# Two unread products at the start, a split gate pair, and a second set of rows turned earlier

## The chip, the cores and the metric

The kernel runs on one core of a Trainium2 chip. A core has a matrix engine (TensorE, PE), a vector engine (VectorE, DVE), a scalar engine (ScalarE, ACT), a general engine (GpSimd, POOL), and a queue engine (SyncE, SP) that mostly issues transfers. Products go to PSUM, a small accumulator memory, and are read from there by VectorE and ScalarE. The metric is the device time of one execution in microseconds (us).

## The reference

Two layers work on x, 8 sequences of 256 rows of 512 numbers, with a context of the same size.

```
x = x + long_convolution(ctx, ctx, layernorm(x))      # 32 heads of 8 x 2 halves, filter of 512
x = x + ternary_ffn(layernorm(x))                     # 512 -> 2048 -> 512, quantised rows and weights
x = x + cross_attention(layernorm(x), ctx)            # 16 heads of 32
x = x + experts(layernorm(x))                         # 2 shared experts, best 2 of 16 routed ones
```

An expert is `w2(gelu(g(x)) * w1(x))` with 256 hidden columns. The router takes the sigmoid of `x @ wa`, keeps the two best experts of each row and weighs their outputs by the two affinities divided by their sum. Everything is float32 apart from the quantised products.

## The kernel before

The program is one long stream for each engine. Inside each stage `in_order` fixes the order of TensorE, VectorE, ScalarE and GpSimd to that of the program text; transfers on SP may be placed by the scheduler. Engines meet through semaphores, and a tile is reused when its last reader is done. A pool's tag with `bufs=n` has n such slots.

**Start.** `first_norm` (L544) takes mean and variance of the first half of the rows, eight tiles of 128 x 512 as they land (`moment`, L149 and L150). Then ScalarE normalises tiles 0 to 3 and VectorE tiles 4 to 7, alternately. PE turns each normalised tile with four 128 x 128 transposes (`transposed`, L162) into a PSUM tile of the tag `tr`, which has two slots. The engine that normalised the tile copies it to `qT` (L537). Up to here PE has had nothing to do. The convolution follows: for each head PE forms `y` (L691) from the filter `tp` and products `kv` of context columns, which GpSimd prepares (L629), and VectorE multiplies and adds.

**Expert stage, shared part.** `gate(tb, e, f, w, k)` (L1468) is half a gate pair: four products of 128 x 512 into a PSUM tile of the tag `gh`, which has four slots. Half 0 is what goes through Gelu, half 1 is the factor. `gated` (L1480) takes the Gelu of half 0 on ScalarE (L1483) and multiplies on VectorE (L1484). tb counts blocks of 512 rows, e the shared experts, f the halves of the hidden columns. `down` (L1488) multiplies back and adds to the rows.

The routing runs in between, as a generator, `route` (L1512), advanced by `next(pieces)`. Its pieces are, in order: the affinities; the best expert; the second best; `both`, the sum of the two choices (L1540); the ranks, where PE counts for each row and expert how many rows came before (17 small products, L1544 to L1550) and VectorE turns counts into places; the slots; then one piece for each of the 16 row tiles. A row piece normalises the tile on VectorE (`dxs`, L1437) and has GpSimd scatter it twice to a table `xd` in HBM (L1600), and scales the rows (L1608). Four pieces have been taken when the loop of the remaining six pairs begins; it does a whole pair, then `gated`, then 2, 3, 3, 3, 3, 2 pieces:

```
    for (tb, e, f), n in zip(rest, (2, 3, 3, 3, 3, 2)):
        gated(tb, e, f, gate_up(tb, e, f, shw[e]), yTs[tb])
```

**Routed part.** A `Unit` (L1625) is one routed expert with up to 256 of its rows. Building it loads its weights and its rows `xr` from `xd` (L1635). The tag `xr` has two slots. `turn` transposes the rows, 8 transposes into two `gh` tiles, and ScalarE copies them to `xT` (L1643). `products` forms the hidden columns (L1656, Gelu L1662, factor L1663), `back` the output (L1672), which goes to a table `yd`. A `Double` (L1681) holds rows of two experts that overflowed; five of them are put among the units, the first at place 3. The loop builds unit i+1, runs the products of unit i, turns unit i+1, then does `back` of unit i-1. Only the first unit is turned ahead of the loop. Afterwards the shared experts of blocks 2 and 3 run while GpSimd gathers rows of `yd`.

Of the kernel before, what the change touches and what calls it, by code (L numbers as in the profile page):

```python
# [8 lines left out]
F32 = mybir.dt.float32  # L9
# [9 lines left out]
B, S, D = 8, 256, 512  # L19
# [59 lines left out]
def tile_kernel(ctx: ExitStack, tc: tile.TileContext, a: dict, out: bass.AP):  # L79
    nc = tc.nc  # L80
# [24 lines left out]
    xs = const.tile([P, 2, B, D], F32, name="xs")  # L105
# [17 lines left out]
    def rsqrt(v, eps, n, name):  # L123

        ve = stat.tile([P, n], F32, tag="rs_ve", name=f"{name}_ve")
        nc.scalar.activation(ve, v, AF.Identity, bias=eps)
        s = stat.tile([P, n], F32, tag="rs_s", name=f"{name}_s")
        nc.scalar.activation(s, v, AF.Sqrt, bias=eps)

        def rest():  # L130
            r0 = stat.tile([P, n], F32, tag="rs_r0", name=f"{name}_r0")
            nc.vector.reciprocal(r0, s)
            return newton(ve, r0, n, name)

        return rest

    def newton(ve, r0, n, name):
        t = stat.tile([P, n], F32, tag="rs_t", name=f"{name}_t")
        nc.vector.tensor_tensor(t, r0, r0, ALU.mult)
        nc.vector.tensor_tensor(t, t, ve, ALU.mult)  # L140
        nc.vector.scalar_tensor_tensor(t, t, -0.5, r0, ALU.mult, ALU.mult)
        r = stat.tile([P, n], F32, tag="rs_r", name=f"{name}_r")
        nc.vector.scalar_tensor_tensor(r, r0, 1.5, t, ALU.mult, ALU.add)
        return r

    def moment(dst, t, name):

        st = stat.tile([P, 6], F32, tag="bn", name=f"{name}_bn")
        nc.vector.bn_stats(st, t)  # L149
        nc.vector.bn_aggr(dst, st)  # L150
# [31 lines left out]
    pp = psA.__enter__()  # L182
# [351 lines left out]
    def turned(xn, nm, t0):  # L534

        ps = transposed(pp, xn, nm, "tr", PERM)
        return lambda copy: copy(qT[:, :, t0 : t0 + P], ps)  # L537

    def minus_mean(mv, r, n, name):
        nmr = stat.tile([P, n], F32, tag="nmr", bufs=2, name=name)  # L540
        nc.vector.scalar_tensor_tensor(nmr, mv[:, :, 0], -1.0, r, ALU.mult, ALU.mult)
        return nmr

    def first_norm():  # L544


        by_act, by_dve = (
            fp.tile([P, 4, D], F32, tag="big", bufs=4, name=f"xn0_{q}") for q in range(2)
        )
        mv = stat.tile([P, B, 2], F32, tag="mv0", bufs=1, name="ln0_mv")  # L550
        for b in range(B):
            moment(mv[:, b, :], xs[:, 0, b, :], f"ln0_{b}")
        r = rsqrt(mv[:, :, 1], ln_eps, B, "ln0")()
        nmr = minus_mean(mv, r, B, "ln0_nmr")
        copies = []
        for i in range(4):
            nc.scalar.activation(
                by_act[:, i, :], xs[:, 0, i, :], AF.Identity, bias=nmr[:, i : i + 1],
                scale=r[:, i : i + 1],
            )  # L560
            copies.append((turned(by_act[:, i, :], f"q0_{i}", i * S), nc.scalar.copy))
            j = 4 + i
            nc.vector.tensor_scalar(
                by_dve[:, i, :], xs[:, 0, j, :], mv[:, j, 0:1], r[:, j : j + 1],
                ALU.subtract, ALU.mult,
            )
            copies.append((turned(by_dve[:, i, :], f"q0_{j}", j * S), nc.vector.tensor_copy))
            if i:
                for _ in range(2):
                    to_place, copy = copies.pop(0)  # L570
                    to_place(copy)
        for to_place, copy in copies:
            to_place(copy)
# [167 lines left out]
    b1c = stat.tile([P, FC], F32, tag="b1c", bufs=1, name="b1c")  # L741
    nc.sync.dma_start(b1c, a["w1b"].rearrange("(p c) -> p c", p=P))
    first_norm()
    following = kv0, rows_of(0, nc.vector.tensor_copy)
    unfinished = None
# [414 lines left out]
    with tc.tile_pool(name="att", bufs=2) as ap_, tc.tile_pool(  # L1160
        name="psC", bufs=2, space=PSUM
# [217 lines left out]
    def weights(names, e, name, gu=None):  # L1379
        if gu is None:  # L1380
            gu = gate_weights(names, e, name)
        w2 = experts.tile([P, EC, D], F32, tag="w2", bufs=4, name=f"{name}_w2")
        nc.sync.dma_start(w2, of_expert(names[2], e).rearrange("(c p) f -> p c f", p=P))
        return gu, w2
# [3 lines left out]
    shw = [weights(shared_names, e, f"s{e}", None if e else gu0) for e in range(SH)]  # L1388
# [79 lines left out]
    def gate(tb, e, f, w, k):  # L1468
        ps = pd.tile([P, TB], F32, tag="gh", name=f"gu{k}{e}_{tb}{f}")
        for c in range(DC):  # L1470
            nc.tensor.matmul(  # L1471
                ps, lhsT=w[0][:, c, k, f * P : (f + 1) * P], rhs=xTs[tb][:, c, :],
                start=(c == 0), stop=(c == DC - 1),
            )
        return ps

    def gate_up(tb, e, f, w):
        return gate(tb, e, f, w, 0), gate(tb, e, f, w, 1)

    def gated(tb, e, f, gu, yT):  # L1480
        gp, up = gu
        ge = mo.tile([P, TB], F32, tag="ge", bufs=2, name=f"ge{e}_{tb}{f}")
        nc.scalar.activation(ge, gp, AF.Gelu, bias=gb[:, e, f : f + 1])  # L1483
        nc.vector.scalar_tensor_tensor(  # L1484
            yT[:, e, f, :], up, eb1[:, e, f : f + 1], ge, ALU.add, ALU.mult
        )
# [12 lines left out]
    def hidden_rows(tb):  # L1499
        return mo.tile([P, SH, EC, TB], F32, tag="yT", bufs=2, name=f"yT_{tb}")  # L1500
# [244 lines left out]
    pieces = route()  # L1745
    yTs = [hidden_rows(tb) for tb in range(2)]
# [5 lines left out]
    first_gate = gate(0, 0, 0, shw[0], 0)  # L1752
# [9 lines left out]
    first_gate = gate(0, 0, 1, shw[0], 0)  # L1762
# [6 lines left out]
    for _ in range(3):  # L1769
        next(pieces)  # L1770
    rest = [(tb, e, f) for tb in range(2) for e in range(SH) for f in range(EC)][2:]
    for (tb, e, f), n in zip(rest, (2, 3, 3, 3, 3, 2)):
        gated(tb, e, f, gate_up(tb, e, f, shw[e]), yTs[tb])
        for _ in range(n):
            next(pieces)

    for tb in range(2):
        for j in range(TB // P):
# [9 lines left out]
    order = [lambda e=e: Unit(f"r{e}", e, NS * P * e, NS * P) for e in range(E)]  # L1788
    for j in range(NO1 // 2):
        order.insert(4 * j + 3, lambda j=j: Double(j))  # L1790
    units = [order[0]()]
    units[0].turn()
    for i in range(len(order)):
        if i + 1 < len(order):
            units.append(order[i + 1]())
        units[i].products()
        if i:
            units[i - 1].turn_back()
        if i + 1 < len(order):
            units[i + 1].turn()  # L1800
        if i:
            units[i - 1].back()
        if i < NTT:
            nc.gpsimd.tensor_tensor(tile_of(i), tile_of(i), srow, ALU.add)
# [15 lines left out]
    shw = [weights(shared_names, e, f"t{e}") for e in range(SH)]  # L1820
# [105 lines left out]
```

## Time and profile before

| what | value |
|---|---|
| runs | 1160.84, 1160.36, 1160.26; median 1160.36 us |
| profiled execution | 1161.17 us, span 1159.4 us |
| mean granted TensorE clock | 0.995 |
| PE busy, 0 to 20.6 us (start) | 5.86 us |
| PE busy, 20.6 to 198 us (convolution) | 169.18 of 177.4 us |
| PE busy, 745 to 860 us (end of attention, shared experts, routing) | 110.44 of 115 us |
| PE busy, 860 to 1070 us (routed experts) | 208.81 of 210 us |

The profile is of one execution. The span runs from the first to the last instruction of the core; the execution's own time is 1.8 us longer. Times inside it count from the start of the span. PE's weight loads are listed apart (PEld) since they overlap products. An f32 product appears as two records, so the four products of half a pair are eight. "Idle before" an instruction is how long its engine had done nothing, and the name behind it is what that instruction waited for last. The chain that ended last is followed back from the end of the program.

### The profile page before, as it was taken

To read this page: it belongs to the slowest core of one execution; us is meant where nothing else is said; L and a number is where in the kernel's file an instruction comes from. 1 tells how busy PE (TensorE), PEld (TensorE's weight loads), DVE (VectorE), ACT (ScalarE), POOL (GpSimd) and SP (SyncE) were. 2 spreads that over 40 slices of the span, in tenths; PEclk is the share of its full clock that TensorE was granted. 3 is DMA by queue.
4 is the path that set the end of the run, shared out by engine and by line. 5 is a ranking of instruction groups with operands and counts; after the bars stand their busy time and mean duration, and the time that the engine had idled before them with its cause. 6 is when DMAs were issued, how large, how long until landed. Compare 5 with 4: busy or idle time off the path is not lost.

```text
span 1159.4 us, 16491 instructions
## 1 busy us (share of the span) xinstructions
PE 1099.6 (95%) x5866; PEld 661.3 (57%) x5885; DVE 679.2 (59%) x1499; ACT 525.3 (45%) x1181; POOL 440.8 (38%) x501
## 2 busy tenths in 40 slices
PE   4999998899988999999999999899999999999997
PEld 3777775454544565555555555554456766675443
DVE  5998999789874565755757656437612122222352
ACT  4437545888883466555556566631011221111000
POOL 5788887144321233333434335312770000000650
PEclk9999999999999999999999999899999999999999
DMA  7424420799400100000000010052667999997571
GB/s 270 153 74 155 145 83 13 255 302 291 116 1 1 55 1 1 20 19 1 20 8 12 2 37 1 1 193 83 238 207 251 312 340 326 294 320 245 153 251 39
DMA packets 122780, 153.25 MB, mean 132 GB/s; under 512 B 7482, under 2 KB 81274, under 8 KB 122179
## 3 DMA queue, kind: packets, MB, share of 16 engines
q1 hardware_dynamic: 108608, 116.49, 31.8%
q10 hardware_dynamic: 8962, 18.85, 4.5%
q0 software_dynamic: 5120, 16.78, 4.3%
q8 instruction: 49, 0.80, 0.3%
q14 instruction: 41, 0.33, 0.1%
HBM read 107.66 MB, written 44.43 MB: 131 GB/s over the span
## 4 chain that ended last, share of the span: by engine, by line
PE 74%; DVE 16%; POOL 4%; ACT 2%; issue 2%; DMA 0%; SPq 0%; POOLq 0%; DVEq 0%; ACTq 0%
PE r_h L1656 10%; PE gu L1471 9%; PE y L691 5%; PE pt L1222 5%; PE fo L1251 5%; PE v_mm L863 5%; PE r_po L1672 5%; PE q_mm L863 5%; PE po L1493 5%; PE k_mm L863 4%; PE sc L1186 2%; PE f_hp L399 2%; PE o L1241 2%; DVE f_hmax L433 2%; PE f_op L471 2%
## 5 line engine op out<-in xcount | busy, mean ns | idle before, releaser
L1211 POOL TENSOR_TENSOR pr<-pr,rden 128x1024 f32<-128x1024 f32 x64 | 121.3, 1895 | 155.2 <-DVE rden L1209 140.0
L691 PE MATMUL y<-kv,tp 128*128 128x288 f32 x640 | 161.7, 408 | 5.2 <-DVE wl L714 5.0
L691 PEld LDWEIGHTS y<-kv,tp 128*128 128x128 f32 x640 | 119.0, 190 | 42.5 <-PE y L691 10.0
L1202 ACT ACTIVATE pr<-sc,mx 128x256 f32<-128x256 f32 x256 | 118.6, 485 | 8.1 <-DVE mx L1194 7.0
L1809 POOL DMA_INDIRECT yg<-yd,slot x32 | 33.4, 1044 | 224.1 <-PE gu L1471 206.3
L1656 PE MATMUL r_h<-r_xT,r_gu 128*128 128x256 f32 x512 | 113.7, 380 | 1.4 <-ACT r_xT L1643 1.4
L1656 PEld LDWEIGHTS r_h<-r_xT,r_gu 128*128 128x128 f32 x512 | 96.8, 190 | 22.4 <-issue 8.0
L1194 DVE TENSOR_REDUCE mx<-sc 128x4 f32<-128x1024 f32 x64 | 77.5, 1213 | 4.8 <-PE sc L1186 4.8
L1222 PE MATMUL pt<-ident,pr 128*128 128x128 f32 x512 | 71.5, 282 | 6.6 <-ACT xT L1281 3.5
L1663 DVE SCALAR_TENSOR_TENSOR r_y<-r_h,eb,r_ge 128x256 f32<-128x256 f32 x32 | 15.5, 484 | 97.3 <-PE r_h L1656 97.3
L1222 PEld LDWEIGHTS pt<-ident,pr 128*128 128x128 f32 x512 | 55.6, 142 | 25.2 <-issue 15.4
L1227 ACT COPY pts<-pt 128x512 f32<-128x512 f32 x64 | 37.9, 592 | 70.1 <-PE pt L1222 70.1
L1662 ACT ACTIVATE r_ge<-r_h,gb 128x256 f32<-128x256 f32 x32 | 15.2, 474 | 108.9 <-PE r_h L1656 108.9
L399 PE MATMUL f_hp<-w1q,f_xq 128*128 128x512 bf16 x245 | 59.4, 379 | 5.3 <-ACT f_xq L376 4.5
L629 POOL TENSOR_TENSOR kv<-kx 128x2048 f32<-128x2048 f32 x16 | 57.6, 3602 | 12.8 <-ACT kx L615 12.8
L1251 PE MATMUL fo<-Wo_sb,oT 128*128 128x512 f32 x128 | 59.3, 607 | 0.0
L863 PE MATMUL k_mm<-Wk_sb,cx 128*128 128x512 f32 x128 | 58.2, 598 | 0.8 <-DVE xs L479 0.8
L471 PE MATMUL f_op<-w2q,f_hq 128*128 128x512 bf16 x249 | 57.7, 382 | 0.5 <-issue 0.2
L863 PE MATMUL v_mm<-Wv_sb,cx 128*128 128x512 f32 x128 | 57.7, 593 | 0.0
L1672 PE MATMUL r_po<-r_w,r_y 128*128 128x512 f32 x128 | 57.7, 593 | 0.0
L863 PE MATMUL q_mm<-Wq_sb,xT 128*128 128x512 f32 x128 | 57.6, 593 | 0.0
L1483 ACT ACTIVATE ge<-gu,gb 128x512 f32<-128x512 f32 x16 | 11.0, 688 | 102.4 <-PE gu L1471 100.0
(486 smaller groups left out, 2108.7 us busy)
## 6 DMA issues: line engine op xcount, KB each, us to landing
xd<-blank SPq DMA_DIRECT2D x1, 15360.0 KB, 59.4
tp<-kpd SPq DMA_DIRECT2D x32, 256.0 KB, 3.3
r_gu<-in_rg SPq DMA_DIRECT2D x16, 512.0 KB, 6.3
r_gu<-in_rw SPq DMA_DIRECT2D x16, 512.0 KB, 6.7
r_w<-in_rw SPq DMA_DIRECT2D x16, 512.0 KB, 6.8
r_xr<-xd SPq DMA_DIRECT2D x16, 512.0 KB, 6.9
yd<-r_yo ACTq DMA_DIRECT2D x32, 256.0 KB, 5.8
yd<-blank SPq DMA_DIRECT2D x1, 6144.0 KB, 78.1
```

Source lines behind the costliest of these rows:

```text
L399: nc.tensor.matmul(dst, lhsT=self.xq[:, i, c, :], rhs=w1q[:, c, cols], start=(c == 0), stop=False)
L471: nc.tensor.matmul(op, lhsT=self.hq[i][:, c, :], rhs=w2q[:, c, :], start=(c == 0), stop=(c == FC - 1))
L691: nc.tensor.matmul(y[:, ll, :, 0:PAIRS], lhsT=tp[:, dl : dl + P], rhs=view(kv, (m0 * G + hh) * PAIRS, [[G * PAIRS, B], [1, PAIRS]]), start ...
L863: nc.tensor.matmul(t, lhsT=lT[:, c, i * P : (i + 1) * P], rhs=w[:, c, :], start=(c == 0), stop=(c == DC - 1),)
L1194: nc.vector.tensor_reduce(self.mx, self.sc.rearrange("p r c k -> p (r c) k"), AX.X, ALU.max, negate=True)
L1202: nc.scalar.activation(self.pr[:, h // 2, h % 2, :], self.sc[:, h // 2, h % 2, :], AF.Exp, bias=self.mx[:, h : h + 1], accum_out=self.den[ ...
L1211: nc.gpsimd.tensor_tensor(flat, flat, rden.unsqueeze(2).to_broadcast([P, 4, S]), ALU.mult)
L1222: nc.tensor.transpose(pt[:, cc, k, :], self.pr[:, rr, cc, k * P : (k + 1) * P], ident)
L1251: nc.tensor.matmul(fo, lhsT=oT[:, c, :], rhs=wsb["Wo"][:, c, :], start=(c == 0), stop=(c == DC - 1))
L1471: nc.tensor.matmul(ps, lhsT=w[0][:, c, k, f * P : (f + 1) * P], rhs=xTs[tb][:, c, :], start=(c == 0), stop=(c == DC - 1),)
L1656: nc.tensor.matmul(ps, lhsT=self.w[0][:, c, k, f * P : (f + 1) * P], rhs=self.xT[:, c, 0:n], start=(c == 0), stop=(c == DC - 1),)
L1672: nc.tensor.matmul(po, lhsT=self.y[:, f, i * P : (i + 1) * P], rhs=self.w[1][:, f, :], start=(f == 0), stop=(f == EC - 1),)
```

## The change

The diff has three parts.

1. In `first_norm`, after the moments of tiles 5 and 6, PE multiplies the two moment columns with the tile of 512 columns, into a PSUM tile of the tag `tr`. Nobody reads the result.
2. In the loop of the remaining pairs the pieces stand between half 0 and half 1 of the pair instead of behind `gated`, and their numbers are 0, 2, 3, 3, 3, 3, and 2 behind the loop. As a result the same pieces come at the same place for VectorE, ScalarE and GpSimd. On PE the ranks now come after half 0 of the pair (0, 1, 1), where before they came ahead of it.
3. The second routed unit is built and turned ahead of the loop, behind the first. In the loop's first pass nothing is built or turned. On PE its transposes move ahead of the first unit's products, on ScalarE its two copies ahead of the first unit's two Gelus. On SP the first gate-weight load of the fourth routed expert comes behind the load of the first `Double`'s rows instead of ahead of it.

```diff
         for b in range(B):
             moment(mv[:, b, :], xs[:, 0, b, :], f"ln0_{b}")
+            if b in (5, 6):
+
+                nc.tensor.matmul(
+                    pp.tile([2, D], F32, tag="tr", name=f"idle{b}"), lhsT=mv[:, b, :],
+                    rhs=xs[:, 0, b, :], start=True, stop=True,
+                )
...
-    for (tb, e, f), n in zip(rest, (2, 3, 3, 3, 3, 2)):
-        gated(tb, e, f, gate_up(tb, e, f, shw[e]), yTs[tb])
+    for (tb, e, f), n in zip(rest, (0, 2, 3, 3, 3, 3)):
+        first_gate = gate(tb, e, f, shw[e], 0)
         for _ in range(n):
             next(pieces)
+        gated(tb, e, f, (first_gate, gate(tb, e, f, shw[e], 1)), yTs[tb])
+    for _ in range(2):
+        next(pieces)
...
-    units = [order[0]()]
-    units[0].turn()
+    units = []
+    for i in range(2):
+        units.append(order[i]())
+        units[i].turn()
     for i in range(len(order)):
-        if i + 1 < len(order):
+        if 0 < i < len(order) - 1:
             units.append(order[i + 1]())
         units[i].products()
         if i:
             units[i - 1].turn_back()
-        if i + 1 < len(order):
+        if 0 < i < len(order) - 1:
             units[i + 1].turn()
```

## The prediction

> **What bounds the kernel now.** I read the page's busy shares first, then the chain that ended last, then TensorE's timeline where the diff touches it, and last the other engines and the clock there.
>
> ```profile
> PE 1099.6 (95%) x5866; PEld 661.3 (57%) x5885; DVE 679.2 (59%) x1499; ACT 525.3 (45%) x1181; POOL 440.8 (38%) x501
> PE 74%; DVE 16%; POOL 4%; ACT 2%; issue 2%; DMA 0%; SPq 0%; POOLq 0%; DVEq 0%; ACTq 0%
> ```
>
> TensorE (PE) is busy for 95% of the span and is 74% of the chain; no DMA is on it. A microsecond taken off PE where the chain runs on PE should therefore come off the end. Rows of that chain in order of time (start, us, what):
>
> ```profile
> 14.36 3.58 PE q L162 x16
> ...
> 20.14 0.66 PE q L162 x4
> 20.80 7.29 PE y L691 x30
> ...
> 873.78 0.87 PE r_xTp L162 x8
> ```
>
> The first 16 transposes take 3.58/16 = 0.22 us each, late ones 0.87/8 = 0.11: PE starts at half speed. TensorE's timeline (start, duration, then idle before and its releaser):
>
> ```profile
> 784.22 7.11 PE L1471 MATMUL gu<-xT,s_gu 128*128 128x512 f32 x16
> 793.18 0.28 PE L1544 MATMUL rank<-both,ones 128*128 128x272 bf16 x1 [1.85 <-DVE both L1540]
> ...
> 794.27 34.50 PE L1471 MATMUL gu<-xT,s_gu 128*128 128x512 f32 x80
> ...
> 857.83 7.17 PE L1656 MATMUL r_h<-r_xT,r_gu 128*128 128x256 f32 x32 [0.72 <-ACT r_xT L1643]
> 864.84 1.04 PE L162 MATMUL r_xTp<-ident,r_xr 128*128 128x128 f32 x8
> 866.61 7.17 PE L1656 MATMUL r_h<-r_xT,r_gu 128*128 128x256 f32 x32 [0.72 <-ACT r_xT L1643]
> ```
>
> PE stands for `both` before the ranks, and twice for ScalarE's copies of turned rows. The granted clock, in windows cut on its own edges (window, length, PE busy, clock, DMA share, GB/s):
>
> ```profile
> 348.60:352.01 3.41, 0.67 (x5) 1.00 0.00 0
> 352.01:355.42 3.41, 3.19 (x15) 0.50 0.00 0
> 737.71:741.13 3.42, 1.67 (x13) 1.00 0.00 0
> 741.13:744.54 3.41, 3.41 (x5) 0.50 0.02 5
> ```
>
> After a thin window the clock is half for exactly one window of 3.413 us. The edges 352.01, 724.06 and 741.13 all lie on one grid; carried back it has edges at 10.68, 14.09 and 17.50. The start's weight loads fall from 0.23 to 0.14 us at about 17.4, so that is the same grid (the clock column reads 1.00 there: it shows no state before its first event).
>
> **Part 1, two products ahead of the first transposes.** They wait for the moments of rows 5 and 6, whose rows end at 9.96 and 10.75. A 128x512 f32 product is 0.86 us at full clock (an output projection's 4 products take 3.44), so 1.72 at half; with that price, of rows with 128 output columns, they run from 10.0 to 13.43. The first transpose at 14.36 is not held up. VectorE gets no wait from them, and their two PSUM slots come free on PE itself. A loss I exclude because of the 0.9 us in between.
>
> What a full clock from 14.36 is worth: VectorE's rows turn one behind the other, since two PSUM slots serve two engines. A warm round is PE 0.66 + copy 0.69 + handovers 0.07 = 1.42. The first of that lane issues at 14.36 + 0.44 = 14.80, the fourth at 14.80 + 3 x 1.42 = 19.06 instead of 20.14: 1.08 saved. A round at half is 1.11 + 0.69 + 0.07 = 1.87 with 0.43 more at either end: all-cold would be 2.2 behind warm. So the bounds are 0 (clock not lifted) and 2.2 (a run whose grid keeps all of this stage cold). With the edges of this run the products fill 2.75 of 3.41 us in the window 10.68 to 14.09. Rises that the trace shows come after 3.14 to 3.41; the clock is kept at 1.38 (222.3 to 225.7), dropped at 2.13 in small products. 2.75 lies nearest to the rises: I take 1.1.
>
> Behind it: the convolution `y` is PE's until 28 us and then alternates with VectorE. The second rows have landed by 21.5 (DMA share 0), are read at 31.0; `tp` and `kgs` are issued when PE or ScalarE frees a slot, so they move along. The third `kv` stands 3.5 us after its input. I let the 1.1 run through.
>
> [...]
>
> **Part 2, ranks between the halves of a pair.** Only four products move on PE: the first half of pair (0,1,1) goes ahead of the ranks. No other engine's order changes. Before: the 16 records of pair (0,1,0) issue until 784.22 + 16 x 0.43 = 791.09, ranks 793.18, next pair 794.27. After: first half 791.09 to 794.53; `both` ended at 793.03, so the ranks go at once, 794.53 to 795.62; second half at 795.62, where it was 794.27 + 3.44 = 797.71. Saved 2.09; the profile's idle of 1.85 (behind a modelled end) is the low bound; I take 2.0.
>
> The price: ranks reach VectorE 1.35 later. Its slots end at 799.81 + 1.35 = 801.16.
>
> ```profile
> 801.42 0.75 DVE L1484 SCALAR_TENSOR_TENSOR yT<-gu,eb,ge 128x512 f32<-128x512 f32 x1 [1.61 <-PE gu L1471]
> ```
>
> Here VectorE idled 1.61 for the second half, which now ends at 799.3, so this product starts at 801.16, 0.26 earlier. The scatters behind it are GpSimd's, 32 at 1.27 us, and keep their time less 0.26. Both PSUM slots the moved half needs were freed by 787.7.
>
> **Part 3, second expert's rows turned behind the first's.** Before: 8 transposes issue in 0.87 (856.07 to 856.94), products at 857.83; again 865.71 to 866.61. After: the second eight fill 856.94 to 857.81 while ScalarE copies the first pair (done 857.79), and the second unit's products follow the first's. Saved 0.89 + 0.90 = 1.79; the idle column gives 2 x 0.72 = 1.44 as the low bound; I take 1.8. ScalarE's two copies (1.07) move ahead of the first Gelu, which waits for PE until 859.87 anyway. The four `gh` slots suffice: the third is needed at 861.2, its copy ends at 858.4.
>
> What parts 2 and 3 need is that the rows are there. PE reaches them at 856.07 - 2.09 = 853.98, the second unit's at 854.85.
>
> ```profile
> 846.60 0.89 SPq L1635 DMA_DIRECT2D r_xr<-xd  x2
> ```
>
> and among the transfers of that stretch, with their median time to landing:
>
> ```profile
> r_xr<-xd SPq DMA_DIRECT2D x2, 512.0 KB, 4.1
> ```
>
> Issued 846.6 and 847.1; the first alone landed 3.6 after, so the second 4.6: 850.2 and 851.7, less 0.26. Some 3 us remain. On SP one load changes place: the fourth routed expert's gate weights go behind the overflow rows `o_xr`, which wait for the second rows' transposes, now at 857.8, still ahead of the end of the first unit's products (864.8) that those weights waited for. They are needed at 895. The units' other loads hang on PE and move with it; PE waits for no DMA from 860 to 1070.
>
> **Sum.** 1.1 + 2.0 + 1.8 = 4.9. The profiled execution took 1161.17 (span 1159.4 and 1.8 around it): it would be 1156.3. It stands 0.8 above the median of the runs, 1160.36, so I predict 1155.5. Low bounds 0 + 1.85 + 1.44 = 3.3 give 1157.1; high ones 2.2 + 2.09 + 1.79 = 6.1 give 1154.3.
>
> [...] A 4-product output projection at 741 took 5.13 on the chain against 3.44: a half-clock window on such work costs 1.7, and one may come or go when the stages shift by 1.1.
>
> **The rivals.**
> - *The clock is not lifted in time* (products of two columns count for little, or 80% of a window is too little): parts 2 and 3 alone, 1160.36 - 3.8 = 1156.6. For it: no rise in the trace after less than 3.14 us. Against: the clock was kept after windows with 1.38 and 1.51 us of busy PE, all of it wide products.
> - *The scatters become the bound*: PE comes earlier but the rows do not, and part 2 is given back: 1157.4. For it: GpSimd issues without a pause until 844.8. Against: 3 us of slack.
> - *Slower*: the second rows, now ahead of the first unit's products, land late and hold everything. PE loses the landing less 854.85; it is as slow as before at a landing of 859.8, and at 862.4 the time is 1163. That is 15 us after issue; the longest of all 16 row loads took 9.1, and 1157 would be the price of that.
> - *The stages take it back*: 28 to 357 us alternates between engines, and thin windows drop the clock. Two more half-clock windows on dense products take 3.4: 1158.9, no change within 0.2%.
>
> **How the numbers follow.** Forecast 0.62, clock not lifted 0.20, scatters 0.07, taken back 0.06, slower 0.05. The forecast's own range is 1154.0 to 1157.0. The first two hold 0.82; with bounds 1154.3 and 1157.1, and part of a half-clock window either way, the range is 1153.5 to 1157.8. A measurement of this kernel tells about 0.2% (2.3 us) from no change: faster is below 1158.0. The first three cases lie below that (0.89, of which 0.01 is left to the noise), the fourth within: faster 0.88, same 0.07, slower 0.05.
>
> **What would show it.** Part 1: weight loads of the first transposes at 0.14 us, q's fourth VectorE tile at 19.1, `y` 1.1 earlier. Part 2: no idle before the ranks, pair (0,1,1) split around them, VectorE's 1.61 gone. Part 3: 16 transposes in a row, no ScalarE wait before either unit's products. Wrong would be: loads still at 0.23 at 14.4; PE idle before `r_xTp` on a DMA; new windows at clock 0.50.

## The result and the profile after

The changed kernel took 1156.40 us (median of 6 runs, 1153.92 to 1157.90) against 1160.31 for the kernel before (6 runs), a ratio of 0.9963 with a 95% interval of 0.9953 to 0.9972: 3.9 us less by the medians, where 4.9 was forecast, and inside the range of 1153.5 to 1157.8. The interval stands for 3.2 to 5.5 us, so it holds the 4.9 too. The profiled execution, the slowest of the six, took 1157.9 (span 1156.1), 3.3 less than the profiled one of before, so it is read against that. The line numbers cited from here on are 6 higher than before behind L552, in every kernel that keeps the products of part 1.

The page of the changed kernel, busy time by engine and the chain by engine:

```profile
PE 1105.1 (96%) x5870; PEld 662.5 (57%) x5889; DVE 679.1 (59%) x1499; ACT 525.2 (45%) x1181; POOL 441.4 (38%) x501
PE 75%; DVE 16%; POOL 3%; ACT 2%; issue 2%; DMA 0%; SPq 0%; POOLq 0%; DVEq 0%; ACTq 0%
```

The bound has not changed: PE carries the chain. PE's timeline of the changed kernel (start, duration, idle before in brackets), at the start, around the ranks, and at the routed rows:

```profile
10.19 3.57 PE L555 MATMUL idle<-xs,ln_mv 128*2 128x512 f32 x4 [10.19 <-DVE ln_mv L150]
14.50 6.72 PE L162 MATMUL q<-ident,xn 128*128 128x128 f32 x32 [0.74 <-issue]
...
784.97 10.55 PE L1477 MATMUL gu<-xT,s_gu 128*128 128x512 f32 x24
795.35 0.28 PE L1550 MATMUL rank<-both,ones 128*128 128x272 bf16 x1
...
796.44 31.06 PE L1477 MATMUL gu<-xT,s_gu 128*128 128x512 f32 x72
827.34 27.63 PE L1499 MATMUL po<-s_w,yT 128*128 128x512 f32 x64
854.81 1.91 PE L162 MATMUL r_xTp<-ident,r_xr 128*128 128x128 f32 x16
856.57 14.08 PE L1662 MATMUL r_h<-r_xT,r_gu 128*128 128x256 f32 x64
```

The ranks stand between two blocks of products with no bracket: the wait of 1.85 for `both` is gone. Sixteen transposes run in a row, the products of both units follow, and the two waits of 0.72 for ScalarE are gone. Nothing waits for the rows.

Where the 3.3 us came from, by starts on PE (before, after): `lgT`, the first transposes for the router, 759.05 and 759.80, a loss of 0.75; the first `r_xTp` 856.07 and 854.81, so a gain of 2.01 between these two; the first `r_po` 874.49 and 871.36, a gain of 1.87 more. The rest of the program ends as much earlier, within 0.14. The start itself lost: `y` begins at 21.06, where it was 20.64. The granted clock of the changed kernel in windows cut on its edges (window, length, PE busy, weight loads, VectorE, ScalarE, GpSimd, clock, DMA share, GB/s):

```profile
8.73:12.14 3.41, 1.95 (x3) 0.34 (x4) 2.86 (x8) 0.32 (x2) 2.71 (x2) 1.00 0.45 160
12.14:15.55 3.41, 2.67 (x7) 1.08 (x6) 1.95 (x8) 1.70 (x3) 0.00 (x0) 1.00 0.98 237
15.55:18.97 3.42, 3.42 (x17) 2.66 (x15) 1.74 (x3) 2.60 (x4) 0.00 (x0) 1.00 0.99 378
...
193.05:196.46 3.41, 1.41 (x13) 0.81 (x11) 3.30 (x11) 1.48 (x3) 2.86 (x13) 1.00 0.01 2
196.46:199.87 3.41, 2.28 (x5) 0.89 (x7) 2.01 (x5) 1.12 (x2) 3.04 (x8) 0.50 0.00 0
199.87:203.29 3.42, 3.42 (x13) 2.33 (x12) 2.69 (x9) 1.43 (x3) 1.48 (x8) 0.50 0.19 23
```

The window of 3.413 us is the same, but its edges are elsewhere: in the profile of before they lie 0.44 after multiples of 3.413 us from the start of the span, here 1.90 after. The transposes' weight loads take 1.57 for eight up to 18.8 and 0.42 for four from 19.12: the clock rose at 18.97, where in before it was 17.50. And two half-clock windows stand behind a thin one at 196.46, where before had none. Between the start and the last microseconds, before has three half-clock windows (from 352.01, 724.06 and 741.13), the changed kernel five (two from 196.46, one from 227.18, two from 353.48).

### The profile page after: what moved, and what is told of

Read it like the earlier page. It is cut to its first block, busy times and chain, and to the rows that moved or that the text cites. A ratio compares the mean times of both kernels' runs of the same rounds, so it can differ in the third digit from the quotient of the medians.

```text
span 1156.1 us, 16504 instructions
## 1 busy us (share of the span) xinstructions
PE 1105.1 (96%) x5870; PEld 662.5 (57%) x5889; DVE 679.1 (59%) x1499; ACT 525.2 (45%) x1181; POOL 441.4 (38%) x501
## 4 chain that ended last, share of the span: by engine, by line
PE 75%; DVE 16%; POOL 3%; ACT 2%; issue 2%; DMA 0%; SPq 0%; POOLq 0%; DVEq 0%; ACTq 0%
PE r_h L1662 10%; PE gu L1477 10%; PE y L697 5%; PE pt L1228 5%; PE v_mm L869 5%; PE r_po L1678 5%; PE q_mm L869 5%; PE fo L1257 5%; PE po L1499 5%; PE k_mm L869 4%; PE sc L1192 2%; PE f_hp L399 2%; PE o L1247 2%; DVE f_hmax L433 2%; PE f_op L471 2%
## 5 line engine op out<-in xcount | busy, mean ns | idle before, releaser
L399 PE MATMUL f_hp<-w1q,f_xq 128*128 128x512 bf16 x245 | 62.5, 394 | 5.5 <-ACT f_xq L376 4.5
```

The costliest lines, as they stand in the source:

```text
L399: nc.tensor.matmul(dst, lhsT=self.xq[:, i, c, :], rhs=w1q[:, c, cols], start=(c == 0), stop=False)
```

## Experiments

Times came in three sets of four kernels. Each set ran on one chip, with the kernel before beside it; the chips of the sets differ. Before took 1160.55 (31 runs), 1161.01 (35) and 1160.40 (29). All ratios are to before in the same set.

### First set: where did part 1 go?

**Parts 2 and 3 alone** (the products of `first_norm` taken out):

```diff
-            if b in (5, 6):
-                nc.tensor.matmul(pp.tile([2, D], ...), lhsT=mv[:, b, :], rhs=xs[:, 0, b, :], ...)
```

> Parts 2 and 3 without the two products at the start. Theory A (the products of two columns never lifted the clock and are worth 0): median as the changed kernel's, 1160.3 - 3.9 = 1156.4 within 0.5. Theory B (they are worth 1.1 in most runs, and the profiled one was an exception of the clock's grid): 1157.5. In the trace: no wait before the ranks, sixteen transposes in a row, and weight loads of the first transposes at 0.23 us until the first edge of the grid that closes a busy window.

1159.87 (1158.22 to 1164.10), ratio 0.9999 [0.9988, 1.0011]. Both expectations missed.

**Part 1 alone**, the rest as before:

> The two products alone. Theory A: 1160.3, no change within 0.5, and the first transposes load their weights in 0.23 us. Theory B: 1159.2, loads at 0.14 us from 14.4 on in most executions.

1159.61 (1157.19 to 1161.51), ratio 0.9993 [0.9985, 1.0002]. In its profile the two products fill a whole clock window (PE's timeline, then the window):

```profile
9.88 3.54 PE L555 MATMUL idle<-xs,ln_mv 128*2 128x512 f32 x4 [9.88 <-DVE ln_mv L150]
14.19 1.06 PE L162 MATMUL q<-ident,xn 128*128 128x128 f32 x8 [0.76 <-issue]
```

```profile
9.85:13.26 3.41, 3.38 (x4) 0.34 (x4) 2.55 (x11) 0.49 (x2) 1.50 (x2) 1.00 0.40 80
```

The first eight transposes take 1.06 for 1.8 or so of before, and `y` begins at 19.41. The trace is theory B's, the time lies between the two theories. Two columns are enough where they fill the window, here 3.38 of 3.41 us; they do because of where it lies.

**Products of 128 columns**, two of them, and behind all eight tiles:

```diff
-pp.tile([2, D], ...), lhsT=mv[:, b, :]
+pp.tile([P, D], ...), lhsT=mv[:, b, 1:2].to_broadcast([P, P])
```

and for the second kernel also

```diff
-            if b in (5, 6):
+            if b >= 0:
```

> The changed kernel, with the two products taken against 128 equal columns (a moment column repeated) instead of 2: same waits, same 512 columns streamed, result still unread. Theory A1 (the monitor counts how much of the array works, two columns are too little): the clock now rises at the first edge after about 13 us, y starts near 20.1, median 1155.3. Theory A2 (2.7 of 3.4 us is too little of a window, whatever the width): as the changed kernel, 1156.4, and the clock rises only at the edge after a window full of transposes.

> The changed kernel, with a 128-column product after each of the eight tiles' moments (unread): PE is busy from about 4.6 us on. A1 and A2 both: at least one whole window is busy before 12, the clock is full at 14.4 at any phase of the grid, weight loads 0.14 us, y starts near 19.9, median 1155.3 or up to 1 lower. If it stays at 0.23 us, neither holds, and PE is late by some 4 us: 1160.

1157.23 (1156.86 to 1161.27), ratio 0.9975 [0.9964, 0.9986], and 1159.04 (1156.18 to 1163.49), 0.9991 [0.9980, 1.0002]. `y` begins at 19.43 and 19.31: the clock is up at the transposes in both (the first eight take 1.06, as with two columns in the run above, where `y` begins at 19.41). Where the products ran through a whole window, columns made no difference; yet a start that is 1.2 us shorter did not make these kernels faster than the changed one had been. Something later took it.

It is found between the ranks and the first `r_xTp`. That stretch is 62.89 us in before; with part 2 the ranks stand half a pair (3.44) later in PE's order, and the changed kernel has 59.46. The profiles of this set have 61.10 (parts 2 and 3), 63.17 and 66.48 (eight and two wide products); part 1 alone, in the order of before, has 62.89. In the three, PE waits in the products `po` of the shared experts for VectorE's sums, which are late, although VectorE stands idle. The profile of the two wide products is that of the slowest of their seven executions (1161.27, the others 1156.86 to 1158.60), so 66.48 is not what most of them had.

### Second set: late sums of VectorE

> The changed kernel once more, beside the single parts on one chip. Two theories of why parts 2 and 3 alone came to 1159.87 instead of 1156.5. L (late VectorE): without the wait before the ranks TensorE reaches the routed rows some 2 us earlier and has no room left when VectorE takes up the sums of the shared experts late (8 us late in those profiles); it can hit every kernel with part 2, so the changed kernel too: median 1157.5 to 1159, a spread of 4 us or more, and from the ranks to the first r_xTp 61 us or more in the profile instead of 59.46. P (part 1 carries it): the late VectorE needs the start without part 1; then again 1156.4 with a spread below 4 us and 59.5 us.

> Part 2 alone. Worth 2.0 us if the wait before the ranks is simply gone: 1158.5 (before taken as 1160.5), no idle time before the ranks, 60.9 from the ranks to r_xTp (62.89 before, less 2.0). By L: 1158.5 at best, median 1159 to 1161, a spread of 4 us or more, with TensorE waiting for VectorE in the products of L1499 or its like. By P the same without part 1: it cannot be better than 1159.5.

> Part 3 alone. 1.8 us: 1158.7; the first routed products follow 16 transposes without the ScalarE wait of 0.72, twice. The order of VectorE and TensorE up to r_xTp is that of before, so by L the room of 2 us is still there and the spread stays at that of before (2.4 us); by P nothing is said of this part.

The edits of part 2 and part 3 alone are those hunks of the diff. The changed kernel took 1159.42 (1155.89 to 1163.76), ratio 0.9983 [0.9966, 0.9999]; part 2 alone 1165.82 (1161.08 to 1170.90), 1.0039 [1.0022, 1.0056], slower than before; part 3 alone 1159.00 (1157.87 to 1162.82), 0.9982 [0.9973, 0.9992]. Theory P falls, since the changed kernel is hit too. L stands in its mechanism, and part 3 is worth 2.0 (0.9 to 3.1). L's sizes were too small: it had 1157.5 to 1159 for the changed kernel and 1159 to 1161 for part 2 alone. One number of the expectation was derived wrongly: part 2 alone should have 62.89 - 3.44 = 59.45 from the ranks to `r_xTp`, not 60.9. It has 65.59.

PE's timeline of the changed kernel in this set:

```profile
824.28 17.57 PE L1499 MATMUL po<-s_w,yT 128*128 128x512 f32 x40
845.86 13.63 PE L1499 MATMUL po<-s_w,yT 128*128 128x512 f32 x24 [4.01 <-DVE over L1620]
859.34 1.91 PE L162 MATMUL r_xTp<-ident,r_xr 128*128 128x128 f32 x16
```

VectorE's in the same run:

```profile
826.94 0.75 DVE L1490 SCALAR_TENSOR_TENSOR yT<-gu,eb,ge 128x512 f32<-128x512 f32 x1 [5.37 <-remote]
...
837.41 0.69 DVE L1503 TENSOR_TENSOR xs<-xs,po 128x512 f32<-128x512 f32 x1 [7.62 <-remote]
...
845.12 0.69 DVE L1503 TENSOR_TENSOR xs<-xs,po 128x512 f32<-128x512 f32 x1 [4.92 <-remote]
```

and the sum that comes first in the profile of the changed kernel shown above:

```profile
830.98 0.69 DVE L1503 TENSOR_TENSOR xs<-xs,po 128x512 f32<-128x512 f32 x1 [0.45 <-PE po L1499]
```

There VectorE has waited 0.45 for the first product and takes it at 830.98, 0.2 after PE has finished it (eight records of 0.43 after 827.34); here it stands idle for 7.62 and starts behind a product that PE finished about 827.7 (eight records of 0.43 after 824.28), and "remote" says that the profile finds nothing that ended its wait. `po` has four slots, so PE can run four products ahead and then stops. Here five products were done when it stopped: the sixth needs the slot of the second, whose sum ends at 845.81, and PE goes on at 845.86 (the profile names `over`, the instruction of VectorE behind that sum). The wait has a second price, in the clock windows of this run:

```profile
841.84:845.25 3.41, 0.01 (x1) 0.00 (x0) 0.13 (x1) 0.00 (x0) 2.90 (x3) 1.00 0.59 222
845.25:848.67 3.42, 2.81 (x4) 1.26 (x5) 3.32 (x7) 0.00 (x0) 2.11 (x1) 0.50 0.12 22
848.67:852.08 3.41, 3.41 (x6) 1.34 (x5) 1.56 (x3) 0.00 (x0) 2.96 (x3) 0.50 1.03 382
```

One empty window, then two at half clock on dense products: the last 24 records of `po` take 13.63, where 24/64 of 27.63 is 10.4. The wait of 4.0 costs 7.6 in all (67.05 against 59.46). Part 2 alone shows the same on PE, a wait of 2.85 and 17.02 for products that take 13.9 elsewhere:

```profile
824.81 13.90 PE L1493 MATMUL po<-s_w,yT 128*128 128x512 f32 x32
841.56 17.02 PE L1493 MATMUL po<-s_w,yT 128*128 128x512 f32 x32 [2.85 <-DVE xs L1497]
```

Part 3 alone has late VectorE too, and loses nothing. PE runs all eight products in one block, and `r_xTp` follows at 855.83 without a wait (PE, then VectorE):

```profile
828.37 27.63 PE L1493 MATMUL po<-s_w,yT 128*128 128x512 f32 x64
```

```profile
835.67 0.75 DVE L1484 SCALAR_TENSOR_TENSOR yT<-gu,eb,ge 128x512 f32<-128x512 f32 x1 [10.01 <-PE po L1493]
...
838.44 0.67 DVE L1497 TENSOR_TENSOR xs<-xs,po 128x512 f32<-128x512 f32 x1
```

The difference is counted from the ranks, on which VectorE's work of this stage hangs. In the order of before PE ends its fourth `po` product 49.3 after the start of the ranks (828.60 + 13.90 - 793.18), with part 2 45.9 (827.34 + 13.90 - 795.35). All eight profiles of the first two sets, against this:

| kernel | first sum after the ranks | fourth `po` ends | lost up to `r_xTp` |
|---|---|---|---|
| changed kernel, first profile | 35.6 | 45.9 | 0 |
| part 1 alone; part 3 alone | 45.5; 45.5 | 49.3 | 0; 0 |
| parts 2 and 3 | 46.5 | 45.9 | 1.6 |
| two, eight wide products | 44.5; 45.9 | 45.9 | 7.0; 3.7 |
| changed kernel again | 45.1 | 45.9 | 7.6 |
| part 2 alone | 48.0 | 45.9 | 6.1 |
| eight narrow products | 45.9 | 45.9 | 3.7 |

A sum lasts 0.7, so one at 45.5 is in time for 49.3 and too late for 45.9. Where the first sum was still in time (44.5 and 45.1), the second came at 53.6 and 52.8, with the fifth product done at 49.3 and 49.6.

**The two-column product behind all eight tiles:**

```diff
-            if b in (5, 6):
+            if b >= 0:
```

> The changed kernel with the same two-column product behind the moments of all eight row tiles instead of two (six products more). If the fullness of the clock's window decides and the columns do not: a whole window of 3.413 us is filled whatever its phase, the first transposes' weight loads take 0.11 to 0.14 us and y begins 19.3 to 19.6 us after the start. If products of two columns count for little: loads of 0.23 and y at 20.6 to 21.1. In time 0.5 to 1.2 less than the changed kernel beside it by the first, equal by the second; L adds its late VectorE to both alike.

1158.46 (1156.32 to 1161.47), ratio 0.9978 [0.9967, 0.9989], 1.0 below the changed kernel of the set, with intervals that overlap, and `y` at 19.50. A window that two-column products filled for 3.31 us raised the clock (at 8.26; the products' weight loads take 0.13 up to 7.36 and 0.09 from 8.67), so the number of columns is not what keeps it low.

### Third set: what makes VectorE late, and does it need to cost?

**No scatters** (the rows are not written to `xd`; the routed experts work on blank rows):

```diff
-            for k in range(2):
+            for k in range(0):
                 ins = nc.gpsimd.indirect_dma_start(
```

**Eight slots for the products of the shared experts**, in the changed kernel, in part 2 alone, and with the eight narrow products:

```diff
-        po = pd.tile([P, D], F32, tag="po", name=f"po{t}")
+        po = pd.tile([P, D], F32, tag=tag, name=f"po{t}")
...
-            down(tb, j, shw, yTs[tb])
+            down(tb, j, shw, yTs[tb], "gh" if j % 2 else "po")
```

> The changed kernel without its 32 scatters of rows (they are left out, so the routed experts work on blank rows); VectorE still writes the rows that they would take. Where the late VectorE comes from: S (the traffic of the scatters, 32 transfers whose landings are announced by all 16 DMA engines) expects VectorE to take the fourth tile's yT within 3 us and every sum of the shared experts within 1 us of TensorE's product, no wait of TensorE between the ranks and r_xTp, 59.5 us between these, and a spread below 4 us around 1156 to 1157. N (something else of this stage, say the code or the signals of TensorE themselves) expects the same 5 to 10 us late yT and first sum, and 61 us or more.

> The changed kernel with the eight products of the shared experts in eight PSUM slots (four of po, four of gh) instead of four, so that TensorE does not need VectorE's sums to go on. C (the late VectorE costs only through these slots, and through the thin window and half clock behind the wait): no wait of TensorE for the sums although VectorE is as late as before, 59.5 us from the ranks to r_xTp, no half clock at 840 to 852, median 1156 to 1157, spread below 4 us. Rival R (late VectorE also makes the scattered rows late, and TensorE then waits for r_xr): 60 to 62 us, a wait before r_xTp for a DMA, median 1158 to 1159.5 as without the slots.

> Part 2 alone with the same eight slots. By C it becomes what part 2 was forecast to be, 2.0 us less than before: 1158.5 to 1159, 60.9 us from the ranks to r_xTp, where part 2 alone with four slots had 1165.8 and 65.6. By R 1160.5 to 1163.

> All parts, the two-column product behind all eight row tiles and the eight slots. By C 0.5 to 1.2 less than the eight slots alone: 1155 to 1156.3, the lowest of all kernels here; y begins 19.3 to 19.6 us after the start. By R no better than 1157.5.

| kernel | time, us | ratio | ranks to `r_xTp` |
|---|---|---|---|
| no scatters | 1156.47 (1155.51 to 1160.11) | 0.9961 [0.9949, 0.9974] | 59.46 |
| eight slots | 1156.48 (1154.46 to 1161.27) | 0.9971 [0.9958, 0.9984] | 59.46 |
| part 2, eight slots | 1158.44 (1157.48 to 1162.86) | 0.9986 [0.9976, 0.9996] | 59.46 |
| eight narrow products, eight slots | 1154.61 (1154.33 to 1155.09, 6 runs) | 0.9947 [0.9934, 0.9961] | 59.46 |

The times are those that S and C expected, but they do not prove them. Part 2 with eight slots, VectorE's timeline:

```profile
829.60 0.69 DVE L1497 TENSOR_TENSOR xs<-xs,po 128x512 f32<-128x512 f32 x1 [0.46 <-PE po L1493]
```

VectorE was not late at all in this set, with all 32 scatters in place: its first sum stands 35.6 after the ranks in all three kernels that have scatters, as in the first profile of the changed kernel. The slots were never needed, and leaving the scatters out removed nothing that the kernels beside it had. What the set does show is part 2 by itself without late sums: 1160.40 - 1158.44 = 1.96 (interval 0.5 to 2.8), with a start that had no products ahead of it. The expected 60.9 repeats the wrong derivation; 59.46 is what no loss looks like. By the medians C's order held for the last kernel too, the fastest of all and faster than C had it. But `y` at 19.3 to 19.6 missed: with the clock low up to 11.20 the eight products ran to 15.26 and held the transposes, which had begun at 14.09 with two (PE's timeline of this last kernel):

```profile
7.03 8.23 PE L555 MATMUL idle<-xs,ln_mv 128*2 128x512 f32 x14 [0.52 <-DVE ln_mv L150]
15.19 1.09 PE L162 MATMUL q<-ident,xn 128*128 128x128 f32 x8
```

`y` began at 20.43, against 20.65 with two products in this set, so its 1.9 us under the eight slots alone are not explained by its profile; the two intervals just touch, and it has six runs. The two profiled executions differ by 0.3 only (1155.43 and 1155.09). All six of the last kernel had a mean granted clock of 0.994 or 0.995, the twelve of the eight slots 0.986 to 0.995, and the three slowest of these (1159.16 to 1161.27) the lowest, 0.986 to 0.988.

Two windows of this set, PE's busy time first: no scatters, then eight slots.

```profile
9.15:12.56 3.41, 2.67 (x4) 0.34 (x4) 2.62 (x9) 0.49 (x2) 2.58 (x2) 1.00 0.43 128
12.56:15.97 3.41, 2.06 (x14) 1.27 (x12) 2.17 (x8) 2.64 (x4) 0.00 (x0) 1.00 0.94 244
```

```profile
11.30:14.71 3.41, 2.67 (x6) 0.78 (x5) 1.97 (x9) 2.01 (x4) 0.14 (x1) 1.00 0.84 219
14.71:18.13 3.42, 3.42 (x17) 2.83 (x16) 1.31 (x3) 2.42 (x4) 0.00 (x0) 1.00 1.01 381
```

Both begin with a window that PE fills for 2.67 us. In the first it holds nothing but the two products, and the clock rose behind it (14 records in the next window's 2.06, `y` at 19.41). In the second it holds the end of the products, a pause of 0.74 and the first transposes, and it rose only a window later (`y` at 20.65).

Busy time alone does not separate the two. Over all half-clock windows of the 14 profiles in which PE worked, each with 3.14 us of busy PE or more was followed by the full clock, and none with 2.49 or less. Between these it went either way: 2.62, 2.67 and 2.80 raised it; 2.62, 2.63, 2.67 (twice), 2.70 and 2.81 did not. Among the last are two-column products alone with a pause of 0.52 (2.63 from 4.38, eight narrow products with eight slots, where the clock rose only at 11.20) and dense products without a pause (2.81 from 845.25, shown above). What decides there is not shown.

## Why the prediction was right, and where it was not

**Part 2, forecast 2.0.** 2.01 between `lgT` and `r_xTp` in the first profile, 1.96 by itself in the third set (0.5 to 2.8). VectorE's slots end at 801.97, and the product that was to start at 801.16, 0.75 later by the loss ahead of it, starts at 801.89 without a wait, where there was one of 1.61.

**Part 3, forecast 1.8.** 1.87 in the profile, 2.0 by itself (0.9 to 3.1).

**The rows.** They were forecast to be there some 3 us ahead. Issued at 847.62 with a median of 4.4 to landing, they are, for PE at 854.81. In no profile does PE wait for them, not even where up to 5.5 us lay between the starts of two scatters (part 2 alone, after 836.73). The 0.26 that the rows were to gain did not come: counted from `lgT` their loads were issued at 87.82, where it was 87.55. The rivals of late rows and of the scatters as the bound fall.

**Part 1, forecast 1.1.** The size was right on average only, and the step behind it was wrong. It took the edges of the profile of before, 10.68 and 14.09, for those of the changed kernel, an assumption that no run shows, and let another grid into its upper bound only. Counted from the start of the span, the 14 profiles have their edges at 14 places, from 0.24 to 3.23 after a multiple of 3.413: 0.44 in before, 1.90 and 2.16 in the two profiles of the changed kernel, 3.02 in part 1 alone. In the first profile the products had 1.95 us of one window and shared the next with a pause and the first transposes, instead of 2.75 in one. So two of the signs that the prediction named for being wrong appeared there: slow weight loads at 14.4, and new windows at clock 0.50.

So part 1 is a matter of luck. The five profiles without any product ahead of the transposes start `y` at 20.64, 20.73, 20.92, 21.12 and 21.83, 21.05 on average. The five with the two narrow ones have 19.30, 19.41 and 19.41, where the clock rose behind them, and 20.65 and 21.06, where it did not: 1.7 earlier or 0.2, and 1.1 on average. By time, part 1 alone gave 0.9, with an interval from -0.2 to 1.7. The first rival, "80% of a window is too little", was half right: at the start 2.62 and 2.67 of 3.41 in the two products raised the clock (77 and 78%), 1.95 (57%) and 2.67 of products and transposes together did not, and neither did 2.63 of narrow products with a pause. The 2.75 of the forecast lies in the stretch from 2.62 to 2.81 where the runs went either way, so "nearest to the rises" was a guess, and that part 1 came to 1.1 on average is luck. It does not hang on two columns against 128: where the products ran through a whole window and ended ahead of the transposes, `y` began at 19.41 and 19.50 with two, at 19.43 and 19.31 with 128.

**The sum.** 4.9 was forecast, 3.9 measured, a gap that the interval of 3.2 to 5.5 does not tell from nothing. In the profiled executions 1.87 and 2.01 arrived in full; the start gave -0.4 and the stages up to the router took another 0.33 (0.75 in all), with a half-clock stretch at 196.46 that before did not have. This is the lottery that the fourth rival named, at a smaller size. From `y` to `lgT`, where all kernels here are alike, the 14 profiles take between 736.54 (part 2 alone) and 738.88 (parts 2 and 3): 2.3 us, more than any one of the parts is worth.

**What the prediction lacked.** It asked what hides behind the ranks for VectorE, and found 0.26 us gained. It did not ask how late VectorE may be before PE stops: that room was 49.3 - 39.1 = 10.2 us before (first sum at 832.24), and is 45.9 - 35.6 = 10.3 in the same quiet conditions, so it looks unchanged. But where VectorE's lateness runs from the ranks and not from PE's products, as in two sets (44.5 to 48.0 in either order), the room shrank by the 3.44 us of the half pair that went ahead. There part 2 alone cost 4.8 us, parts 2 and 3 together were worth 0.7 (interval -1.3 to 1.4), and the whole change 1.6 (0.1 to 3.9). The sums and the waits of eight profiles fit this count; it was not tested by giving the late sums more room. The result of 3.9 holds where VectorE is not late. None of the rivals, the one on the slower side included, was this mechanism.

**What stays open.** What delays VectorE. It went with the set of runs, each on a chip of its own, and not with the kernel: late in eight of eight profiles of two sets, in none of four of the third, nor in the first profiles of both kernels. In the late ones the trace also lacks about half of the updates of the eight semaphores on which GpSimd's transfers end: 473 to 593 are recorded, and 1048 in each of the others that have the scatters (in before 1024 of these are landings, 16 for each of the 32 scatters and 32 gathers). What that has to do with the lateness, no run here shows. Every execution here has its span and granted clock on record, so none tells what a kernel takes without any recording. Whether the eight slots protect against late sums was not tested, since they met none.

## What to carry to other kernels

Count the room behind a buffer from the event on which the late engine's work hangs, not from the engine that fills it: moving work ahead of a wait saves the wait (here 2.0) and takes the length of that work (here 3.44) from every cover that is counted from the waiting work. Products nobody reads warmed a cold matrix engine here (`y` began at 19.30 to 19.50 in six of nine profiles with them, and at 20.64 to 21.83 in the five without), but the clock's window lay elsewhere in each of the 14 profiles; to rely on it the products must fill a window wherever it lies (from 3.14 of 3.41 us on the clock rose every time, from 2.62 to 2.81 only sometimes), and must end before the real work is ready (eight of them ran to 15.26 in one kernel, and `y` began at 20.43). A short stall on a dense stretch was paid twice where it left a clock window nearly empty: with 0.01 us of busy PE in a window, a wait of 4.0 cost 7.6.

## What the hardware showed that was not expected

- The phase of the 3.413 us clock window differs between all 14 profiles (0.24 to 3.23, as above), and in the first six executions of the changed kernel the time goes with the mean granted clock: 1153.92 at 0.995, 1155.64 at 0.994, 1156.30 to 1156.56 at 0.993 and 1157.90 at 0.991. Beside the single parts, with late sums, it does so less (1155.89 and 1159.42 both at 0.994).
- After one thin window the clock was low for two windows, not for exactly one as the prediction read it, in the changed kernel's first profile (196.46 to 203.29, behind 1.41 us of busy PE) and in its second (845.25 to 852.08, behind 0.01). In both the first of the two was not full either (2.28 and 2.81); in before the low windows held 3.19 or 3.41 and were single.
- Products of two output columns raised the clock (3.38 of 3.41 us from 9.85 in part 1 alone) like those of 128 (from 9.90 to 13.64 in the two wide ones), with 1.06 for the first eight transposes behind both. A window of transposes alone raised it too (3.42 of 3.42 us from 15.55 in the changed kernel, 3.14 from 14.09 in before).
- VectorE started 5 to 9 us after all that the profile shows it to wait for was done (4.92 and 7.62 in the changed kernel's second profile, 9.02 in part 2 alone). Two sets of runs show late sums in every profile; a third, on another chip, shows them in none.
